# Two depthwise filters moved to 32x32 diagonal products on TensorE, in a layout of four bands of rows

## The chip, the cores and the metric

The kernel runs on one core of one Trainium2 chip. A core has TensorE (a matrix array that writes to PSUM), VectorE, ScalarE and GpSimd for elementwise work, and a sync queue that issues DMA transfers. In the profile they are PE (its weight loads PEld), DVE, ACT, POOL and SP. PSUM has eight banks of 512 f32 per partition. The metric is device time in microseconds (us), the median of several executions.

## The reference, cut to what matters

The input is 32 images of 56x56 pixels with 96 channels, f32. Four layers follow each other:

```python
# layer 0: mixture of 4 experts, weights mixed per image
h = relu(bn(x @ Wk + ...))             # 96 -> 384 channels
h = relu(bn(depthwise3x3(h) + ...))    # 384 channels
x = bn(h @ Wk2 + ...) + x              # 384 -> 96
# layer 1: depthwise 5x5 of 96 channels, added to its input
x = x + depthwise5x5(x, kernel)
# layer 2: relu, depthwise 3x3 of 96 channels, 96x96 product, batch norm
y = depthwise3x3(relu(x), dw_kernel) + dw_bias
x = bn(y @ pw_kernel + pw_bias)
# layer 3: shifted-window attention (7x7 windows, 3 heads of 32), then a
# perceptron 96 -> 384 -> 96 with gelu; layer norm before each, residual after
```

The change touches layers 1 and 2. A depthwise filter has no sum over channels: each channel is filtered by itself. On TensorE it can be written as one product per tap with a diagonal weight matrix, summed in PSUM.

## The kernel before

Each step of the outer loop works on three images at once; the generators hand over to each other at `yield`, in the proportion of their weights, and the scheduler places the instructions in that order of priority:

```python
for step in range(B + 2):
    # attention and perceptron of image step-2, weight 107
    # layers 1 and 2 of image step-1,           weight 44
    # layer 0 of image step,                    weight 42
    interleave(stages)
```

Layer 0 filters its 384 channels on VectorE, in six blocks (two halves of the rows, three groups of 128 channels):

```python
for t in range(9):                     # L320 on
    view = h1[:, dy : dy + HALF, dx : dx + W]
    if t == 0:
        nc.vector.tensor_scalar(acc, view, tap, None, ALU.mult)               # L324
    else:
        nc.vector.scalar_tensor_tensor(acc, view, tap, acc, ALU.mult, ALU.add)  # L326
nc.scalar.activation(h2[:, k], h2[:, k], AF.Relu, ...)                        # L329
```

After three blocks it makes the 384 -> 96 product (L344) and writes the image, with a border of zeros, to `x1`. Layers 1 and 2 of the image before it are then:

```python
def conv5(i):                          # 8 rows of layer 1
    pt = mm.tile([P, 512], F32, tag="mm", name="pt")
    o = pt[:C, : 8 * W].rearrange("c (r w) -> c r w", w=W)
    for t in range(25):
        dy, dx = divmod(t, 5)
        nc.tensor.matmul(o, diag5[:, t],                     # L368; diag5[:, t] is 96x96
                         x1[:, 8 * i + dy : 8 * i + dy + 8, dx : dx + W],
                         start=(t == 0), stop=(t == 24))
        if t % 5 == 4 and t < 24:
            yield
    nc.scalar.activation(x2[:, 1 + 8 * i : 9 + 8 * i, 1 : 1 + W], o, AF.Relu)   # L377

def filtered(i):                       # 7 rows of layer 2, on VectorE
    ...
    for t in range(9):
        if t == 0:
            nc.vector.tensor_scalar(acc, view, tap, None, ALU.mult)              # L390
        else:
            nc.vector.scalar_tensor_tensor(acc, view, tap, acc, ALU.mult, ALU.add)  # L392
    nc.gpsimd.tensor_copy(d[:, :, W:], d[:, :, :3])                              # L393
    nc.scalar.copy(dp, d[:, :, 3:].rearrange("c r (j w) -> c j r w", w=14))      # L395

def pointwise():                       # the 96x96 product and the bias
    ...                                # L402 on TensorE, L409 on VectorE
```

Attention works on eight groups of seven rows. For each group, `project` makes queries, keys and values (L478 to L490), `scores` takes three PSUM banks at once (L504), `probabilities` adds the mask on VectorE (L510), takes exponentials on ScalarE (L517) and divides on GpSimd (L521), `turned` transposes (L528), `weighted` multiplies with the values (L546), `attended` projects and adds (L554, L557). The perceptron follows (L570 to L585), and 17 output transfers a row group on the sync queue (L592 to L599). PSUM is shared out so:

```python
mm = ctx.enter_context(tc.tile_pool(name="mm", bufs=4, space=PSUM))    # all else
att = ctx.enter_context(tc.tile_pool(name="att", bufs=3, space=PSUM))  # scores, turned; and 1 "po"
```

Of the kernel before, what the change touches and what calls it, by code (L numbers as in the profile page):

```python
# [18 lines left out]
C = 96  # L19
# [7 lines left out]
NP = 4  # L27
NH = 3
# [30 lines left out]
def kernel(ctx: ExitStack, tc: tile.TileContext, a: dict, mask: bass.AP, out: bass.AP):  # L59
# [10 lines left out]
    att = ctx.enter_context(tc.tile_pool(name="att", bufs=3, space=PSUM))  # L70
# [4 lines left out]
    ones = const.tile([P, P], F32, name="ones")  # L75
# [83 lines left out]

    k5 = load([C, 25], a["L1_conv_kernel"].rearrange("c a b -> c (a b)"), "k5")  # L160
    nc.vector.tensor_scalar(k5[:, 12:13], k5[:, 12:13], 1.0, None, ALU.add)
    diag5 = const.tile([C, 25, C], F32, name="diag5")
    for t in range(25):
        nc.vector.tensor_scalar(diag5[:, t], ident[:C, :C], k5[:, t : t + 1], None, ALU.mult)
# [13 lines left out]
    nc.vector.tensor_scalar(dwb, ones[:C], col(U_DWB), None, ALU.mult)  # L178
# [22 lines left out]
    x2 = big.tile([C, H + 2, W + 2], F32, name="x2")  # L201
    nc.gpsimd.memset(x1, 0.0)
    nc.gpsimd.memset(x2, 0.0)


    consumed = [H]

    def stage_conditional(b):
# [5 lines left out]
        def load_rows(i):  # L214
            xin = work.tile([PK, NP, C], F32, tag="xin", name="xin", bufs=3)
            nc.sync.dma_start(
                out=xin,
                in_=x[b, 7 * i : 7 * i + 7].rearrange("r w c -> (r w) c").rearrange("(p j) c -> p j c", j=NP),
            )
            loaded.append(xin)  # L220
# [4 lines left out]
        for i in range(NROW):  # L225
            if i + 2 < NROW:
                load_rows(i + 2)
            xin = loaded[i]
            pt = mm.tile([P, 512], F32, tag="mm", name="pt")
            for j in range(NP):  # L230
                nc.tensor.transpose(pt[:C, j * PK : (j + 1) * PK], xin[:, j], ident[:PK, :PK])
            nc.scalar.activation(
                xT[:, i * RT : (i + 1) * RT].rearrange("c (p j) -> c j p", j=NP),
                pt[:C, :RT].rearrange("c (j p) -> c j p", j=NP),
                AF.Copy,
                accum_out=sums[:, i : i + 1],
            )
            yield
# [5 lines left out]
        nc.vector.tensor_scalar(pooled_w, ones[:C], pooled, 1.0 / (H * W), ALU.mult, ALU.mult)  # L244
# [69 lines left out]
        for at, (half, k) in enumerate(blocks):  # L314
# [22 lines left out]
            for n in range(4):  # L337
                r = half * HALF + 7 * n

                while consumed[0] < r + 7:  # L340
                    yield
# [19 lines left out]
    def stage_depthwise(b, res):  # L361

        def conv5(i):
            pt = mm.tile([P, 512], F32, tag="mm", name="pt")
            o = pt[:C, : 8 * W].rearrange("c (r w) -> c r w", w=W)
            for t in range(25):
                dy, dx = divmod(t, 5)
                nc.tensor.matmul(  # L368
                    o,
                    diag5[:, t],  # L370
                    x1[:, 8 * i + dy : 8 * i + dy + 8, dx : dx + W],
                    start=(t == 0),
                    stop=(t == 24),
                )
                if t % 5 == 4 and t < 24:
                    yield
            nc.scalar.activation(x2[:, 1 + 8 * i : 9 + 8 * i, 1 : 1 + W], o, AF.Relu)  # L377

        def filtered(i):
            d = work.tile([C, 7, W + 3], F32, tag="d", name="d")  # L380
            first = 7 * i + 3
            parts = ((0, first, 7),) if i < NROW - 1 else ((0, first, 4), (4, 0, 3))
            for to, r, n in parts:
                acc = d[:, to : to + n, :W]
                for t in range(9):
                    dy, dx = divmod(t, 3)
                    tap = col(U_DWK + t)
                    view = x2[:, r + dy : r + dy + n, dx : dx + W]
                    if t == 0:
                        nc.vector.tensor_scalar(acc, view, tap, None, ALU.mult)  # L390
                    else:
                        nc.vector.scalar_tensor_tensor(acc, view, tap, acc, ALU.mult, ALU.add)  # L392
            nc.gpsimd.tensor_copy(d[:, :, W:], d[:, :, :3])  # L393
            dp = work.tile([C, NP, 7, 14], F32, tag="dp", name="dp", bufs=1)
            nc.scalar.copy(dp, d[:, :, 3:].rearrange("c r (j w) -> c j r w", w=14))  # L395
            packed.append((i, dp))

        def pointwise():
            i, dp = packed.pop()
            pt = mm.tile([P, 512], F32, tag="mm", name="pt")  # L400
            for j in range(NP):
                nc.tensor.matmul(  # L402
                    pt[:PK, j * C : (j + 1) * C],
                    dp[:, j].rearrange("c r w -> c (r w)"),
                    pw,
                    start=True,
                    stop=True,
                )
            nc.vector.tensor_tensor(  # L409
                res[:, i],  # L410
                pt[:PK, : NP * C].rearrange("p (j c) -> p j c", c=C),
                bias2[:PK, None, :].to_broadcast([PK, NP, C]),
                ALU.add,
            )


        packed = []
        done = 0
        for i in range(7):
            for n, _ in enumerate(conv5(i)):  # L420
                yield
                if n == 1 and packed:
                    pointwise()

                    if 7 * done + 10 < 8 * i:
                        filtered(done)
                        done += 1
            consumed[0] = 8 * i + 6
            if packed:
                pointwise()  # L430
            if 7 * done + 10 < 8 * i + 8:
                filtered(done)
                done += 1
            yield
        consumed[0] = H
        while packed:
            for _ in range(4):
                yield
            pointwise()
            if done < NROW:  # L440
                filtered(done)
                done += 1
        assert done == NROW
# [25 lines left out]
    def stage_swin(b, res):  # L469
# [26 lines left out]
        def scores(i):  # L496

            qT, kT = rows_of[i][:2]
            pss = [att.tile([P, 512], F32, tag="att", name="ps") for _ in range(NH)]
# [7 lines left out]
        def probabilities(i, h):  # L507
            ps = scored[i][h]
            s = work.tile([PK, NP, PK], F32, tag="s", name="s", bufs=6)
# [14 lines left out]
        def turned(i, h):  # L524
            s = probs.pop((i, h))
            ps = att.tile([P, 512], F32, tag="att", name="ps")
# [9 lines left out]
        def weighted(i):  # L536

            v = rows_of[i][2]
            po = att.tile([P, 512], F32, tag="po", name="po", bufs=1)
# [105 lines left out]
    for step in range(B + 2):  # L645
# [3 lines left out]
        if 0 <= step - 1 < B:  # L649
            consumed[0] = 0  # L650
            residuals[step - 1] = two.tile([PK, NROW, NP, C], F32, tag="res", name="res")
            stages.append((stage_depthwise(step - 1, residuals[step - 1]), 44))
# [5 lines left out]
def build(nc, shapes, batch):  # L658

    a = {k: nc.dram_tensor(f"in_{k}", s, F32, kind="ExternalInput").ap() for k, s in shapes.items()}  # L660
    mask = nc.dram_tensor("in_mask", (2, PK, NP, PK), F32, kind="ExternalInput").ap()
    out = nc.dram_tensor("out", (batch, H, W, C), F32, kind="ExternalOutput").ap()
    with tile.TileContext(nc) as tc:
        kernel(tc, a, mask, out)
# [13 lines left out]
```

## Time and profile before

The time before is 9404.55 us (three runs, 9403.75 to 9406.23). The profiled execution spans 9402.1 us at a mean granted TensorE clock of 0.959.

| engine | busy us | share of the span | instructions |
|---|---|---|---|
| TensorE, products | 8762.3 | 93% | 47622 |
| TensorE, weight loads | 4987.7 | 53% | 47622 |
| VectorE | 7190.0 | 76% | 11221 |
| ScalarE | 4176.0 | 44% | 11520 |
| GpSimd | 3782.1 | 40% | 3406 |

Busy time is the time in which at least one instruction of the engine ran; loads overlap products. The chain of waits follows the program back from its last instruction, at each step to what released it, and says what share of the span each engine and line had on it. In a group line the figures after the bar are the busy time, the mean duration of one instruction in ns, and the idle time of the engine just before such instructions. One matrix product of f32 leaves two records of each kind. A steady step, from one image's first input transpose to the next one's, takes 287 us.

### The profile page before, as it was taken

Reading aid. Unit: us, or ns where it says so; the run is one execution under the profiler, and the core shown is the slowest. Engines: PE = TensorE matmul, PEld = TensorE weight load, DVE = VectorE, ACT = ScalarE, POOL = GpSimd, SP = SyncE. Lnnn points to the kernel's source line nnn. Section 1 sums busy time; section 2 is a strip of 40 time slices with the busy share of each in tenths; the row PEclk is TensorE's granted clock in tenths of the full one; section 3 lists DMA queues with packets and bytes.
Section 4 is the critical chain, followed back from the end, with each engine's and each line's share of the span. In section 5 each row is a group of like instructions: output and inputs, shape, how many; then the busy total and the mean of one; then the engine's idle time right before and its main releaser. Section 6 shows DMA issues by size and latency. Waiting matters only on the chain.

```text
span 9402.1 us, 132043 instructions
## 1 busy us (share of the span) xinstructions
PE 8762.3 (93%) x47622; PEld 4987.7 (53%) x47622; DVE 7190.0 (76%) x11221; ACT 4176.0 (44%) x11520; POOL 3782.1 (40%) x3406
## 2 busy tenths in 40 slices
PE   5899999999999999999999999999999999999998
PEld 2455555555555555555555555555555555555555
DVE  5778777788777787777887777877778877778754
ACT  2344444444444444444444444444444444444434
POOL 2244344444343443444443434434444434444333
PEclk8999999999999999999999999999999999999997
DMA  0000000000000000000000000000000000000000
GB/s 23 6 10 5 8 11 11 11 7 7 9 11 11 10 6 8 11 11 11 7 7 9 11 11 11 5 8 11 11 11 7 7 9 11 11 11 6 5 6 11
DMA packets 164927, 88.07 MB, mean 9 GB/s; under 512 B 138455, under 2 KB 164272, under 8 KB 164272
## 3 DMA queue, kind: packets, MB, share of 16 engines
q1 hardware_dynamic: 164272, 79.62, 3.3%
q8 instruction: 376, 6.16, 0.3%
q14 instruction: 279, 2.29, 0.1%
HBM read 40.95 MB, written 38.54 MB: 8 GB/s over the span
## 4 chain that ended last, share of the span: by engine, by line
PE 59%; DVE 26%; ACT 5%; POOL 4%; issue 3%; SPq 2%; DMA 0%; DVEq 0%; POOLq 0%; ACTq 0%
PE pt L368 30%; DVE h L326 18%; PE pt L344 5%; PE pt L577 4%; PE pt L570 4%; DVE d L392 2%; ACT s L517 2%; PE ps L504 2%; PE pt L402 2%; PE po L546 2%; PE pt L478 2%; PE pt L487 2%; PE pt L482 2%; PE pt L554 1%; PE ps L528 1%
## 5 line engine op out<-in xcount | busy, mean ns | idle before, releaser
L368 PE MATMUL pt<-x,diag 96*96 96x448 f32 x11200 | 4598.5, 552 | 44.6 <-ACT h L300 44.6
L326 DVE SCALAR_TENSOR_TENSOR h<-h,mix,h 128x1568 f32<-128x1568 f32 x1536 | 2840.7, 1860 | 4.3
L368 PEld LDWEIGHTS pt<-x,diag 96*96 96x96 f32 x11200 | 1742.6, 165 | 2000.9 <-issue 1898.8
L521 POOL TENSOR_TENSOR s<-s,den 98x392 f32<-98x392 f32 x768 | 996.1, 1299 | 1367.2 <-DVE den L520 1358.1
L392 DVE SCALAR_TENSOR_TENSOR d<-x,c,d 96x392 f32<-96x392 f32 (+2 forms) x2304 | 1446.6, 645 | 7.6 <-ACT x L377 1.3
L517 ACT ACTIVATE s<-s,top 98x98 f32<-98x98 f32 x3072 | 1118.1, 368 | 420.6 <-DVE top L514 420.0
L563 POOL TENSOR_TENSOR tb<-res,L_conv_b 98x384 f32<-98x384 f32 x256 | 655.7, 2561 | 1075.7 <-DVE res L557 678.4
L84 POOL TENSOR_TENSOR var<-var,mhalf 98x4 f32<-98x4 f32 x512 | 685.0, 1338 | 445.0 <-DVE var L83 427.7
L577 PEld LDWEIGHTS pt<-w,hid 128*98 128x98 f32 x6144 | 689.5, 189 | 207.9 <-ACT hid L571 117.2
L577 PE MATMUL pt<-w,hid 128*98 128x96 f32 x6144 | 710.7, 274 | 84.2 <-ACT hid L571 84.2
L492 POOL TENSOR_TENSOR xb<-res,L_conv_bo 98x384 f32<-98x384 f32 x256 | 386.7, 1511 | 833.7 <-DVE res L557 700.2
L570 PE MATMUL pt<-hT,w 96*128 96x392 f32 x1536 | 615.0, 540 | 106.4 <-ACT hT L466 106.4
L344 PE MATMUL pt<-h,wmix 128*96 128x392 f32 x1536 | 574.1, 504 | 60.6 <-ACT h L329 37.4
L293 PE MATMUL pt<-xT,wmix 96*128 96x392 f32 (+1 forms) x1536 | 591.2, 519 | 28.6 <-ACT h L300 24.4
L300 ACT ACTIVATE h<-pt,bias,s 128x392 f32<-128x392 f32 (+1 forms) x768 | 491.4, 686 | 272.3 <-PE pt L293 247.1
L466 ACT ACTIVATE hT<-pt,c 96x392 f32<-96x392 f32 x512 | 343.1, 670 | 593.2 <-PE pt L464 592.9
L517 ACT ACTIVATION_READ_ACCUMULATOR s<-s,top 98x1 f32 x3072 | 586.7, 191 | 0.0
L571 ACT ACTIVATE hid<-pt,c 128x392 f32<-128x392 f32 x768 | 444.3, 585 | 249.0 <-PE pt L570 215.9
L451 DVE TENSOR_TENSOR lnd<-res,mu 98x384 f32<-98x384 f32 x512 | 380.2, 743 | 218.4 <-PE pt L464 179.0
L457 POOL TENSOR_TENSOR lnd<-lnd,var 98x384 f32<-98x384 f32 x512 | 531.0, 1037 | 40.2
L510 DVE TENSOR_TENSOR s<-ps,masks 98x392 f32<-98x392 f32 x768 | 410.9, 553 | 177.2 <-PE ps L504 177.2
L329 ACT ACTIVATE h<-h,biasd,s 128x1568 f32<-128x1568 f32 x192 | 325.2, 1694 | 438.0 <-DVE h L326 438.0
(112 smaller groups left out, 10152.3 us busy)
## 6 DMA issues: line engine op xcount, KB each, us to landing
xin<-in_x SPq DMA_DIRECT2D x256, 147.0 KB
out<-o SPq DMA_DIRECT2D x1792, 4.1 KB
out<-o SPq DMA_DIRECT2D x1792, 1.1 KB
out<-o SPq DMA_DIRECT2D x672, 36.8 KB
out<-o SPq DMA_DIRECT2D x96, 21.0 KB
out<-o SPq DMA_DIRECT2D x96, 15.8 KB
wpw<-in_L_conv_Wpw SPq DMA_DIRECT2D x1, 576.0 KB
wpwl<-in_L_conv_Wpwl SPq DMA_DIRECT2D x4, 144.0 KB
```

The source lines that it names most:

```text
L84: nc.gpsimd.tensor_tensor(dst, dst, mhalf[:n, : dst.shape[1]], ALU.pow)
L293: nc.tensor.matmul(pt[:, : n * W], wmix[:, k * P : (k + 1) * P], xT[:, (first + r) * W : (first + r + n) * W], start=True, stop=True,)
L326: nc.vector.scalar_tensor_tensor(acc, view, tap, acc, ALU.mult, ALU.add)
L344: nc.tensor.matmul(pt[:C, :RT], wmix2[:, q * C : (q + 1) * C], h2[:, q, n * RT : (n + 1) * RT], start=(q == 0), stop=(q == NB - 1),)
L368: nc.tensor.matmul(o, diag5[:, t], x1[:, 8 * i + dy : 8 * i + dy + 8, dx : dx + W], start=(t == 0), stop=(t == 24),)
L392: nc.vector.scalar_tensor_tensor(acc, view, tap, acc, ALU.mult, ALU.add)
L457: nc.gpsimd.tensor_tensor(d, d, var[:, :, None].to_broadcast([PK, NP, C]), ALU.mult)
L517: nc.scalar.activation(s[:, j], s[:, j], AF.Exp, bias=top[:, j : j + 1], accum_out=den[:, j : j + 1])
L521: nc.gpsimd.tensor_tensor(s, s, den[:, :, None].to_broadcast([PK, NP, PK]), ALU.mult)
L563: nc.gpsimd.tensor_tensor(tb, res[:, i], b2[:PK, None, :].to_broadcast([PK, NP, C]), ALU.add)
L570: nc.tensor.matmul(pt[:, :RT], w1[:, k * P : (k + 1) * P], hT, start=True, stop=True)
L577: nc.tensor.matmul(pt[:PK, j * C : (j + 1) * C], hidden[k][:, j * PK : (j + 1) * PK], w2[:, k], start=(k == 0), stop=(k == NB - 1),)
```

## The change

It gives each 32x32 block of the matrix array its own small diagonal product, and lets the array hold twelve of them at a time. Layer 1 keeps its input `x1` with 96 channels on 96 partitions (three groups of 32). Its output goes to a new layout: the image is cut into four bands of 14 rows, and band b of each channel group goes to partitions 32b to 32b+31. So twelve products (three channel groups by four bands) use twelve blocks of the array. Layer 2 reads this layout, band by band, and brings the result back to 96 partitions, again with twelve blocks. Between the two, the rows at the band edges are copied to the neighbouring band by two DMA transfers. VectorE no longer takes part in the filter of layer 2. What it is for is to use the array's rows and columns, of which a 96x96 diagonal matrix uses only the diagonal, and to relieve VectorE.

The PSUM pools are cut anew: four banks for the filters, four for everything else, attention included. Layer 0 may write `x1` only when all of layer 1 is done, the weight of the middle stage falls from 44 to 26, and some buffers shrink (`xin` from 3 to 2, `s` from 6 to 5).

```diff
-    att = ctx.enter_context(tc.tile_pool(name="att", bufs=3, space=PSUM))
+    cv = ctx.enter_context(tc.tile_pool(name="cv", bufs=4, space=PSUM))
...
-    diag5 = const.tile([C, 25, C], F32, name="diag5")
+    diag5 = const.tile([C, 25, 32], F32, name="diag5")
...
-    x2 = big.tile([C, H + 2, W + 2], F32, name="x2")
+    x2 = big.tile([P, NG, BAND + 2, W + 2], F32, name="x2")
+    filtered = big.tile([C, NP, H + 3, 14], F32, name="filtered")
...
-                while consumed[0] < r + 7:
+                while not consumed[0]:
...
-        def conv5(i): ...
-        def filtered(i): ...
+        for u in range(2):
+            banks = [cv.tile([P, 512], F32, tag="cv", name="pc") for _ in range(NG)]
             for t in range(25):
                 dy, dx = divmod(t, 5)
+                for band in range(NBAND):
+                    r = BAND * band + 7 * u + dy
+                    for g in range(NG):
+                        gs = slice(32 * g, 32 * g + 32)
+                        nc.tensor.matmul(
+                            rows(banks[g], P)[32 * band : 32 * band + 32],
+                            diag5[gs, t],
+                            x1[gs, r : r + 7, dx : dx + W],
+                            start=(t == 0), stop=(t == 24),
+                        )
                 if t % 5 == 4 and t < 24:
                     yield
+            for g in range(NG):
+                nc.scalar.activation(x2[:, g, 1 + 7 * u : 8 + 7 * u, 1 : 1 + W], rows(banks[g], P), AF.Relu)
+            yield
+        consumed[0] = True
+        nc.sync.dma_start(out=x2[32:, :, 0], in_=x2[: P - 32, :, BAND])
+        nc.sync.dma_start(out=x2[: P - 32, :, BAND + 1], in_=x2[32:, :, 1])
+        for u in range(2):
+            banks = [cv.tile([P, 512], F32, tag="cv", name="pc") for _ in range(NBAND)]
+            for t in range(9):
+                ...
+                for g in range(NG):
+                    for band in range(NBAND):
+                        nc.tensor.matmul(
+                            rows(banks[band], P)[32 * g : 32 * g + 32],
+                            diag3[bs, g, t],
+                            x2[bs, g, r : r + 7, dx : dx + W],
+                            start=(t == 0), stop=(t == 8),
+                        )
+                if t % 3 == 2 and t < 8:
+                    yield
+            for band in range(NBAND):
+                ...                     # three nc.scalar.copy from banks[band] to filtered
+            yield
+        nc.gpsimd.tensor_copy(filtered[:, :, H:], filtered[:, :, :3])
+        yield
+        for i in range(NROW):           # the pointwise product, a yield after each
...
-            pss = [att.tile([P, 512], F32, tag="att", name="ps") for _ in range(NH)]
+            pss = [mm.tile([P, 512], F32, tag="mm", name="ps") for _ in range(NH)]
...
-            stages.append((stage_depthwise(step - 1, residuals[step - 1]), 44))
+            stages.append((stage_depthwise(step - 1, residuals[step - 1]), 26))
```

## The prediction

> **What bounds the kernel now.** I read the busy line first, then the chain of waits, then the costliest groups, then the time by stretches of one step. A step is one turn of the outer loop: attention and perceptron of image b-2, the two filters of image b-1, the first layer of image b.
>
> ```profile
> PE 8762.3 (93%) x47622; PEld 4987.7 (53%) x47622; DVE 7190.0 (76%) x11221; ACT 4176.0 (44%) x11520; POOL 3782.1 (40%) x3406
> ...
> PE 59%; DVE 26%; ACT 5%; POOL 4%; issue 3%; SPq 2%; DMA 0%; DVEq 0%; POOLq 0%; ACTq 0%
> PE pt L368 30%; DVE h L326 18%; PE pt L344 5%; PE pt L577 4%; PE pt L570 4%; DVE d L392 2%; ACT s L517 2%; PE ps L504 2%; PE pt L402 2%; PE po L546 2%; PE pt L478 2%; PE pt L487 2%; PE pt L482 2%; PE pt L554 1%; PE ps L528 1%
> ...
> L368 PE MATMUL pt<-x,diag 96*96 96x448 f32 x11200 | 4598.5, 552 | 44.6 <-ACT h L300 44.6
> L326 DVE SCALAR_TENSOR_TENSOR h<-h,mix,h 128x1568 f32<-128x1568 f32 x1536 | 2840.7, 1860 | 4.3
> ...
> L392 DVE SCALAR_TENSOR_TENSOR d<-x,c,d 96x392 f32<-96x392 f32 (+2 forms) x2304 | 1446.6, 645 | 7.6 <-ACT x L377 1.3
> ```
>
> TensorE is busy 93% and its layer-1 filter (L368) alone is 30% of the chain. But VectorE is second with 26%, nearly all of it the first layer's depthwise filter (L326), which the change leaves alone. The layer-2 filter that does leave VectorE (L392) is only 2% of the chain. So the bound changes hands within a step. The stretches show that (columns: stretch, length, then busy time and count of each engine, then granted TensorE clock, DMA share and GB/s):
>
> ```profile
> 28.00:167.00 139.00, 59.70 (x153) 30.22 (x152) 100.11 (x81) 37.05 (x55) 20.49 (x27) 0.74 0.03 9
> 167.00:380.00 213.00, 183.77 (x562) 85.61 (x561) 150.64 (x189) 48.41 (x76) 54.90 (x43) 0.91 0.02 6
> 4688.00:4736.00 48.00, 47.59 (x297) 26.50 (x296) 21.12 (x50) 29.29 (x109) 14.21 (x16) 1.00 0.09 26
> 4736.00:4901.00 165.00, 158.31 (x838) 83.78 (x837) 150.41 (x208) 72.84 (x205) 63.29 (x55) 0.98 0.00 1
> 4901.00:4975.00 74.00, 65.92 (x355) 44.73 (x355) 53.10 (x92) 28.24 (x49) 41.40 (x35) 0.92 0.07 17
> 8997.00:9224.00 227.00, 222.34 (x1336) 128.27 (x1336) 122.83 (x271) 92.89 (x303) 68.89 (x77) 0.99 0.02 5
> 9224.00:9402.00 178.00, 136.53 (x934) 101.65 (x932) 69.61 (x163) 84.72 (x285) 60.58 (x67) 0.65 0.04 9
> ```
>
> Rows 3 to 5 are one full step, 287 us: its start is TensorE alone, its middle has TensorE at 96% and VectorE at 91%, its end has neither full. Row 1 is the first layer alone (139 us, and VectorE-heavy), row 2 first layer and filters, row 6 filters and attention, row 7 attention and perceptron alone: 178 us although no engine is over 77%.
>
> **What the Trainium skill says.** Three places bear on it, and one warns. "TensorEngine Tiling (Array Packing)", Key Properties: different tiles load weights and multiply in parallel. "TensorE: Matmul & The Clock Gate", Measured speedup vs the span model: sixteen 32x32 tiles together ran 10.6 times as fast as one after another. The trace before agrees for three tiles, side by side in columns (L546) and in rows (L504):
>
> ```profile
> 5001.65 0.88 PE L546 MATMUL po<-pT,v 98*32 98x98 f32 x24
> 5002.45 4.03 PE L368 MATMUL pt<-x,diag 96*96 96x448 f32 x10
> ...
> 5007.44 0.94 PE L504 MATMUL ps<-kT,qT 32*98 32x98 f32 x24
> ```
>
> Each f32 product leaves two records. Ten L368 records run from 5002.45 to the next line's start at 5006.32, so one takes 387 ns, 0.864 ns a column. The 24 records of L546 are eight groups of three over 98 columns; the last lasts some 250 ns, so seven intervals fill 0.63 us: 90 ns, 0.92 ns a column for three tiles at once. Three tiles cost what one does. Twelve at once (rows times columns) no run here shows. Gotcha 1: PSUM Pressure, of the first page, says that row tiles must not write one PSUM bank together; the change gives each row group its own bank. The clock page's section What's actually happening warns that the clock halves when the array idles: row 7 shows 0.65, the full step 1.00 to 0.92.
>
> **The change part by part, per image.**
>
> 1. Layer-1 filter. Out: 4598.5/32 = 143.7 us of TensorE. In: 25 taps x 2 half-bands x 2 records = 100 waves of twelve tiles over 392 columns. At 0.864 x 392 = 339 ns a wave, 33.9 us.
> 2. Layer-2 filter. Out of VectorE: L392 1446.6 and its first tap L390 (165.8 in the groups by shape), together 1612/32 = 50.4 us. In on TensorE: 9 x 2 x 2 = 36 waves, 12.2 us. For filling and draining I add 0.25 us (one record's tail) for each of 16 bursts: 4 us.
> 3. ScalarE. Out: the relu L377 and the copy L395, (120.6+137.6)/32 = 8.1 us. In: six relus of 392 at about 0.6 (L300's 392 takes 0.69, L533's copy 0.48) and 24 copies, eight of 294 elements at 0.45 and sixteen of at most 77 at 0.33 (estimates from L533 and L517's 368 ns for 98): 12.5 us. Net +4.
> 4. Two halo transfers an image. The copies they need come after the last relu, and the program order has a projection, transposes and weighted sums on TensorE between the last layer-1 product and the first that waits for them. I count 0 to 3 us.
> 5. PSUM. Scores, transposes and weighted sums lose their four banks and share four with everything else; the filters take the other four.
>
> Sums of one step: TensorE 271.8-143.7+50 = 178 us, VectorE 224.6-50.4 = 174, ScalarE 130+4 = 135. If these overlapped perfectly the step would be near 180. They can't, because VectorE's L326 and L324, (2840.7+197.0)/32 = 95 us, stand in two clumps. So I dealt out the turns that the three generators take (107, 44, 42 before; 107, 26, 42 after), gave each turn the busy time of its rows, and cut the step by what the first layer does: A loading, B first three channel blocks, C outputs, D the other three blocks, E outputs and the rest. TensorE/VectorE in us, scaled by 0.90 and 0.93 so that the sums before are the measured busy times:
>
> - before: A 74/40, B 62/73, C 46/24, D 56/70, E 33/16. The larger ones add up to 296; measured 287, so the rule reads 3% high.
> - after: A 51/35, B 42/61, C 23/12 (ScalarE 26 is the largest), D 34/61, E 34/11. The larger ones: 51+61+26+61+34 = 233, less 3% = 226.
>
> To that I add 5 us, my choice, for shared PSUM and for waits that layer-1 products used to cover: **231 us a step**. The whole: 167 to the end of the first image's first layer (start 28 + row 1, unchanged); the next step 150 (row 1 plus a little, its 213 was TensorE); 30 full steps x 231 = 6930; filters with attention 180 (row 7's length, as TensorE's 222 falls by 94); row 7 unchanged 178. Sum 7605, rounded to **7600 us**.
>
> **Rivals.**
>
> - *VectorE becomes the bound and hides most of the gain.* This is part of my sum: B and D stay at 61 each. If all slack of TensorE were gained and VectorE never waited, a step would be 190 and the whole about 6400. Against that speaks row 7: attention alone is held by its own chain of waits.
> - *Twelve tiles don't run together.* If only six did, the filters would take 46 us more on TensorE; that falls on A and C, 25 to 35 us a step, whole about 8500. If only three did, the filters would cost about as much as before, and only VectorE's 50 us would be won: 9000 or a little over. For it: nothing here shows more than three. Against it: rows and columns each show no loss at three, and the skill's sixteen.
> - *PSUM becomes the wait.* One step takes about 185 tiles from those four banks (96 in attention, 40 in the perceptron, 41 in the first layer, 8 in the pointwise product). In 231 us that is 5.0 us a tile; a tile needs about 0.7 of writing and 0.6 of reading, plus its wait behind VectorE's operations of 1.86 us. Three banks at once for scores make it tight. A further 20 us a step would give 8200.
> - *The clock halves.* TensorE will be full about 77% of a step. In B and D a halved clock would be hidden behind VectorE, in A and E not: up to 15 us a step.
> - *Output issues on the sync queue.* A row group's 17 output transfers hold that queue 7.8 us, so 62 us an image; the perceptron's stretch is 74 us. It can shrink little, and my E and D together (95 us) leave room.
>
> **Range and chances.** A step of 213 (little loss to PSUM, some smoothing across the parts) gives about 7050; one of 252 (PSUM and clock both bite, or tiles overlap in part) about 8250. Faster by over 2% would fail only if tiles ran three or four at a time: 0.04 slower, 0.03 the same, 0.93 faster.
>
> **What would show each step right or wrong.** The new filter lines on TensorE should be busy about 1100 and 390 us, together under 1700; over 2500 would mean that tiles queue. VectorE should be busy near 5580. In a full step VectorE should be near 100% in two stretches of some 60 us, and on the chain L326's successor should lead, with over 25%. If waits of TensorE for VectorE's mask addition or copies lead the waits, PSUM is the rival that won; if the clock in full steps is under 0.85, the clock is. The prediction is wrong altogether if a wave of twelve takes far more than 339 ns.

## The result and the profile after

The changed kernel takes **9085.8 us** (9082.6 to 9091.9, four runs) against 9404.3 (9403.8 to 9406.2, four runs): 0.966 of the time before, interval 0.9645 to 0.9678. The gain is 319 us. Predicted was 7600, with 8250 as the upper end of the range, so more than four fifths of the expected gain are missing.

The page of the changed kernel has these lines in the places of those shown of before: busy time, chain by engine, chain by line, and three of the costliest groups. In the new file L347 is layer 0's taps (before L326), L396 the layer-1 products (before L368), and L423 the layer-2 products, which take the place of VectorE's L392.

```profile
PE 7756.6 (85%) x88646; PEld 4572.9 (50%) x88646; DVE 5804.0 (64%) x8611; ACT 4125.0 (45%) x12000; POOL 3442.0 (38%) x3182
...
PE 48%; DVE 31%; ACT 11%; POOL 4%; issue 4%; SPq 1%; DMA 0%; ACTq 0%; DVEq 0%; POOLq 0%
DVE h L347 21%; PE pc L396 11%; PE pt L588 7%; ACT s L535 6%; PE pt L365 5%; PE pt L595 5%; PE pc L423 3%; PE pt L314 3%; DVE s L528 2%; POOL var L87 2%; PE pt L572 2%; PE pt L505 2%; PE pt L496 2%; DVE h L345 2%; PE pt L448 2%
...
L347 DVE SCALAR_TENSOR_TENSOR h<-h,mix,h 128x1568 f32<-128x1568 f32 x1536 | 2889.5, 1903 | 5.2 <-DVE den L538 0.5
L396 PE MATMUL pc<-x,diag 32*32 32x392 f32 x38400 | 2109.7, 572 | 11.7 <-ACT x L406 6.6
...
L423 PE MATMUL pc<-x,diag 32*32 32x392 f32 x13824 | 711.8, 573 | 6.0 <-ACT filtered L440 3.8
```

VectorE fell by 1386 us, as it should (5804; predicted 5580). TensorE fell by only 1006, although the filters were to save some 3000. Two readings follow from these lines. First, the filters are busy 2109.7 + 711.8 = 2822 us, 88 us an image and not 50. Second, take the filters off the engine's sum: (7756.6 - 2821.5)/32 = **154 us** an image of other products, where before it was (8762.3 - 4598.5)/32 = **130 us**. The change doesn't touch those products, and they cost 24 us more.

Where in the run the prediction missed is in the stretches (stretch, length, busy time and count of each engine, granted clock, DMA share, GB/s). The rows are the first image's layer 0, the second step, 30 full steps, and the end:

```profile
28.00:161.50 133.50, 54.17 (x152) 26.69 (x150) 100.20 (x81) 37.37 (x55) 16.64 (x26) 0.73 0.03 9
161.50:332.00 170.50, 120.78 (x1949) 69.45 (x1947) 110.86 (x108) 46.08 (x91) 44.47 (x38) 0.82 0.03 9
332.00:8694.00 8362.00, 7249.00 (x82946) 4248.51 (x82945) 5431.06 (x8028) 3856.96 (x11241) 3232.75 (x2957) 0.85 0.04 11
8694.00:9090.00 396.00, 330.63 (x3602) 226.63 (x3600) 156.39 (x365) 183.32 (x614) 129.97 (x143) 0.77 0.04 9
```

The steps hold nearly the whole miss: 8362 where 30 x 231 = 6930 was predicted. The start is 332 for 317 and the end 396 for 358. So the question is one step: 279 us for 231.

One full step of before, then one of after, each cut as in the prediction into A to E (loading, three blocks of taps, layer 0's outputs, three blocks, the rest). The second and fourth number of a row's busy times are weight loads and ScalarE, the fifth GpSimd:

```profile
4687.70:4749.30 61.60, 61.13 (x374) 33.67 (x373) 34.42 (x87) 33.26 (x116) 15.84 (x18) 1.00 0.07 21
4749.30:4822.40 73.10, 69.29 (x369) 36.98 (x368) 70.28 (x80) 35.72 (x109) 31.60 (x24) 0.95 0.00 1
4822.40:4859.50 37.10, 37.02 (x207) 19.55 (x206) 27.43 (x60) 17.50 (x65) 16.97 (x20) 1.00 0.00 0
4859.50:4926.60 67.10, 61.25 (x313) 35.67 (x310) 63.99 (x60) 25.56 (x39) 29.13 (x20) 0.97 0.02 5
4926.60:4976.30 49.70, 44.73 (x233) 29.87 (x234) 28.52 (x66) 18.33 (x34) 25.35 (x26) 0.90 0.08 19
```

```profile
4796.10:4856.90 60.80, 59.24 (x995) 35.84 (x994) 28.63 (x77) 33.48 (x119) 16.40 (x19) 0.92 0.09 24
4856.90:4919.10 62.20, 52.52 (x610) 25.72 (x609) 58.15 (x57) 26.39 (x75) 26.49 (x21) 0.73 0.01 2
4919.10:4967.30 48.20, 43.86 (x565) 24.01 (x566) 18.21 (x43) 26.12 (x106) 16.03 (x19) 0.89 0.01 2
4967.30:5036.90 69.60, 48.76 (x307) 32.63 (x306) 61.55 (x57) 27.45 (x53) 30.57 (x23) 0.81 0.04 9
5036.90:5076.00 39.10, 38.94 (x302) 24.08 (x301) 14.67 (x38) 15.43 (x27) 18.49 (x19) 0.94 0.07 16
```

Of the parts, only B is as predicted (62 for 61). A is 10 us too long, C 22, D 9 and E 5. In A, C and E TensorE is busy 91 to 100% of the time, so there the miss is TensorE's. In B and D VectorE is busy 93 and 88%, and it is there that the granted clock drops most: 0.73 and 0.81, where before it was 0.95 and 0.97.

### The profile page after: what moved, and what is told of

Read it like the earlier page. It is cut to its first block, busy times and chain, and to the rows that moved or that the text cites. A ratio compares the mean times of both kernels' runs of the same rounds, so it can differ in the third digit from the quotient of the medians.

```text
span 9090.1 us, 213022 instructions
## 1 busy us (share of the span) xinstructions
PE 7756.6 (85%) x88646; PEld 4572.9 (50%) x88646; DVE 5804.0 (64%) x8611; ACT 4125.0 (45%) x12000; POOL 3442.0 (38%) x3182
## 4 chain that ended last, share of the span: by engine, by line
PE 48%; DVE 31%; ACT 11%; POOL 4%; issue 4%; SPq 1%; DMA 0%; ACTq 0%; DVEq 0%; POOLq 0%
DVE h L347 21%; PE pc L396 11%; PE pt L588 7%; ACT s L535 6%; PE pt L365 5%; PE pt L595 5%; PE pc L423 3%; PE pt L314 3%; DVE s L528 2%; POOL var L87 2%; PE pt L572 2%; PE pt L505 2%; PE pt L496 2%; DVE h L345 2%; PE pt L448 2%
## 5 line engine op out<-in xcount | busy, mean ns | idle before, releaser
L347 DVE SCALAR_TENSOR_TENSOR h<-h,mix,h 128x1568 f32<-128x1568 f32 x1536 | 2889.5, 1903 | 5.2 <-DVE den L538 0.5
L396 PE MATMUL pc<-x,diag 32*32 32x392 f32 x38400 | 2109.7, 572 | 11.7 <-ACT x L406 6.6
L396 PEld LDWEIGHTS pc<-x,diag 32*32 32x32 f32 x38400 | 875.4, 113 | 689.2 <-issue 449.0
L87 POOL TENSOR_TENSOR var<-var,mhalf 98x4 f32<-98x4 f32 x512 | 747.0, 1459 | 937.0 <-DVE var L86 878.9
L588 PE MATMUL pt<-hT,w 96*128 96x392 f32 x1536 | 758.9, 643 | 121.8 <-ACT hT L484 121.7
L314 PE MATMUL pt<-xT,wmix 96*128 96x392 f32 (+1 forms) x1536 | 708.4, 590 | 130.3 <-DVE res L575 56.0
L365 PE MATMUL pt<-h,wmix 128*96 128x392 f32 x1536 | 628.2, 546 | 122.6 <-ACT pT L551 67.0
L423 PE MATMUL pc<-x,diag 32*32 32x392 f32 x13824 | 711.8, 573 | 6.0 <-ACT filtered L440 3.8
L581 POOL TENSOR_TENSOR tb<-res,L_conv_b 98x384 f32<-98x384 f32 x256 | 510.3, 1993 | 483.1 <-DVE res L575 381.4
L321 ACT ACTIVATE h<-pt,bias,s 128x392 f32<-128x392 f32 (+1 forms) x768 | 481.9, 691 | 393.7 <-PE pt L314 388.5
L575 DVE TENSOR_TENSOR res<-pt,xb 98x384 f32<-98x384 f32 x256 | 141.3, 552 | 801.0 <-PE pt L572 801.0
L510 POOL TENSOR_TENSOR xb<-res,L_conv_bo 98x384 f32<-98x384 f32 x256 | 332.2, 1298 | 844.2 <-DVE res L575 649.9
L350 ACT ACTIVATE h<-h,biasd,s 128x1568 f32<-128x1568 f32 x192 | 324.4, 1690 | 646.3 <-DVE h L347 646.3
L588 PEld LDWEIGHTS pt<-hT,w 96*128 96x128 f32 x1536 | 345.2, 239 | 421.1 <-ACT hT L484 183.4
```

The costliest lines, as they stand in the source:

```text
L87: nc.gpsimd.tensor_tensor(dst, dst, mhalf[:n, : dst.shape[1]], ALU.pow)
L314: nc.tensor.matmul(pt[:, : n * W], wmix[:, k * P : (k + 1) * P], xT[:, (first + r) * W : (first + r + n) * W], start=True, stop=True,)
L365: nc.tensor.matmul(pt[:C, :RT], wmix2[:, q * C : (q + 1) * C], h2[:, q, n * RT : (n + 1) * RT], start=(q == 0), stop=(q == NB - 1),)
L396: nc.tensor.matmul(rows(banks[g], P)[32 * band : 32 * band + 32], diag5[gs, t], x1[gs, r : r + 7, dx : dx + W], start=(t == 0), stop=(t == ...
L423: nc.tensor.matmul(rows(banks[band], P)[32 * g : 32 * g + 32], diag3[bs, g, t], x2[bs, g, r : r + 7, dx : dx + W], start=(t == 0), stop=(t ...
L581: nc.gpsimd.tensor_tensor(tb, res[:, i], b2[:PK, None, :].to_broadcast([PK, NP, C]), ALU.add)
```

## The experiments

Three explanations of the missing gain were on the table: PSUM's shared banks, the twelve tiles and the order of the products, and TensorE's clock together with VectorE's clump of taps. All times but those of the two kernels and of the last version are one execution each; executions of one kernel agree within 0.3% here, so differences under 30 us are not read.

### PSUM: the bank layout without the new filters

The kernel before, with attention's banks merged into the shared pool and the layer-1 filter given four banks of its own, as the change divides them:

```diff
-    att = ctx.enter_context(tc.tile_pool(name="att", bufs=3, space=PSUM))
+    cv = ctx.enter_context(tc.tile_pool(name="cv", bufs=4, space=PSUM))
-            pss = [att.tile([P, 512], F32, tag="att", name="ps") for _ in range(NH)]
+            pss = [mm.tile([P, 512], F32, tag="mm", name="ps") for _ in range(NH)]
...                        # ps and po in the same way; the layer-1 filter's pt from cv
```

> The kernel before, with only the PSUM split of the change: scores, transposes and weighted sums share the four banks of everything else, the 96x96 filter of layer 1 has four banks of its own. Nothing is left out. If the shared banks are what ate the gain (theory PSUM), some 20 to 40 us a step are lost here too: 10000 to 10600 us. If the gain was lost to lone products and the order on TensorE (theory order), or to the clock, this stays within 2% of before: 9300 to 9600 us.

Measured 9225.9 us: 178 us *faster* than before, outside both expected ranges. In the kernel before, the new division costs nothing on balance. Of the 319 us that the whole change wins, the re-division of banks would have won 178; the step went from 287 to about 283 us and the second step from 213 to 170. If the two parts simply add, the new filters themselves won some 140.

It does not follow that shared banks cost nothing in the changed kernel. TensorE's longest wait there, and the next, are:

```profile
PE pt L572 <- ACT h L321: 261.2, 30, 8.7
PE po L564 <- DVE pT L549: 221.4, 60, 6.6
```

The first comes once a step and is a wait for a shared bank, as part D of the step above shows on TensorE and ScalarE:

```profile
4979.35 1.68 PE L314 MATMUL pt<-xT,wmix 96*128 96x448 f32 x4
...
4982.66 1.63 PE L314 MATMUL pt<-xT,wmix 96*128 96x392 f32 x4
4993.01 1.64 PE L572 MATMUL pt<-wo,oT 96*98 96x96 f32 x8 [8.72 <-ACT h L321]
...
4982.84 0.48 ACT L569 COPY oT<-po 96x392 f32<-96x392 f32 x1 [4.11 <-PE po L564]
4990.65 1.69 ACT L350 ACTIVATE h<-h,biasd,s 128x1568 f32<-128x1568 f32 x1 [7.33 <-DVE h L347]
4992.25 2.41 ACT L321 ACTIVATE h<-pt,bias,s 128x448 f32<-128x448 f32 x4
```

Layer 0's four products (L314, two records each) fill all four banks. ScalarE reads them (L321) only after its instruction in front of that (L350) has waited 7.33 us for VectorE's taps. Attention's output product (L572) has had its operand since 4983.3 and waits 8.72 us for a bank. In the run of this experiment, with the 96x96 filter, the two longest such waits add up to 55 and 36 us. So the rival of PSUM is refuted as a cost of the bank division by itself, not as a wait in the changed kernel; what one bank more would win there no run shows.

### The filters: what is left when they are nearly gone

One tap of each filter (leaves out 24 of 25 and 8 of 9), in the scheduler's order; the stage still hands over as often as before:

```diff
-            for t in range(25):
+            for t in (12,):
...
-            for t in range(9):
+            for t in (4,):
```

> The changed kernel with one tap of 25 in layer 1 and one of 9 in layer 2; the other 24 and 8 are left out, everything else stays, so 88 us a step of TensorE's filter work fall to some 4 to 6. Theory order (the filter products, in pieces, are still on the path): at least 30 us a step less, under 8200 us. Theory PSUM or a VectorE and attention chain that holds the step: the filters are off the path already, and it stays over 8700 us.

Measured 8375.5 us, between the two expectations, clock 0.703:

```profile
PE 6442.9 (77%) x39494; PEld 4129.3 (49%) x39494; DVE 5755.2 (69%) x8611; ACT 4124.6 (49%) x12000; POOL 3676.8 (44%) x3182
```

The filters' busy time fell from 88 to 19 us an image, 69 less; a steady step fell from 279 to 257, 22 less. The other products grew in the same run: (6442.9 - 618.0)/32 = 182 us, after 154. This is the run that pointed to the clock.

### The order of the products

In the scheduler's order the bursts of the filters don't stay whole. The timeline of the changed kernel on TensorE shows what that costs (start, length, line, count of records; each product leaves two):

```profile
4797.69 3.80 PE L396 MATMUL pc<-x,diag 32*32 32x392 f32 x116
4801.42 0.54 PE L482 MATMUL pt<-ident,lnd 98*96 98x98 f32 x4
4801.79 0.50 PE L250 MATMUL pt<-ident,xin 98*96 98x98 f32 x4
4802.22 0.84 PE L396 MATMUL pc<-x,diag 32*32 32x392 f32 x2
...
4875.07 1.51 PE L396 MATMUL pc<-x,diag 32*32 32x392 f32 x2
...
4877.95 6.79 PE L396 MATMUL pc<-x,diag 32*32 32x392 f32 x118
```

A piece of 116 records takes 3.73 us up to the next line's start, 32 ns a record. One product (two records) that the scheduler dealt out alone takes 0.84 us, as much as 26 records in a burst. The last two rows are the same two things at half clock: 1.51 and 6.79. Counted from the starts of all records, an image has 25 such small pieces (102 records of 1632), and they take 25 us of TensorE, idle time left out.

To keep the bursts whole, TensorE's instructions were held to the order in which the program emits them:

```diff
-        interleave(stages)
+        with tc.manual_schedule(engines={mybir.EngineType.PE}):
+            interleave(stages)
```

> The changed kernel with TensorE's instructions held to the order in which the program emits them, so that bursts of 60 and 36 products stay whole and no product of a filter stands alone; all other engines are ordered by the scheduler. Theory order: the filters fall from 88 us a step to 50 to 60, lone products vanish, 15 to 30 us a step are won: 8150 to 8600 us. Theory PSUM or clock: within 2% of 9086, or slower, since a fixed order can make TensorE wait.

> Control: the kernel before with TensorE held to the emitted order in the same way. If a fixed order is good in itself, this wins as much as the changed kernel does with it. Theory order says that only packed products suffer from being pulled apart (a lone one takes as long as twelve), so this stays within 2% of 9404: 9250 to 9600 us.

Measured 8893.0 us for the changed kernel, 193 less, and 9916.2 for the kernel before, 512 more. Both missed their ranges: the first won 7 us a step where order alone was to win 15 to 30, the second lost over 5% where it was to stay within 2. So it isn't that this order is good in itself: it is worse for the kernel before, and better for the one whose packed bursts the scheduler splits.

```profile
L396 PE MATMUL pc<-x,diag 32*32 32x392 f32 x38400 | 1644.8, 568 | 48.2 <-POOL x L374 48.2
...
L423 PE MATMUL pc<-x,diag 32*32 32x392 f32 x13824 | 634.8, 625 | 24.4 <-DMA x<-x 19.9
```

The filters fell from 88 to (1644.8 + 634.8)/32 = 71 us an image, the others stayed (157). TensorE has 14 us less to do, and a steady step is only 7 shorter (279 to 272).

Larger and smaller pieces, both with TensorE in emitted order: all 25 taps in one burst of 300 products (layer 2's nine in one of 108), or one tap (12 products) at a time with the stage's weight raised to match.

```diff
-                if t % 5 == 4 and t < 24:
-                    yield
+                if t == 24:            # the large pieces; the small ones: if t < 24: yield
+                    for _ in range(4):
+                        yield
```

> As a_pe, with the filters in bursts as long as they can be: all 25 taps of a half band (300 products, some 17 us at 28 ns a record) and all 9 taps of layer 2 (108, 6 us) without a break; the number of turns is the same. The other end from a_fine_pe (12 products; 9762 us, clock 0.741). The filters' own time falls from 73 us a step to 50 to 55. Theory burst length: fewer starts, and the array is warm within a burst: 8400 to 8850 us. Theory clock: between the bursts there is nothing left to hold the clock, it falls below 0.80, and what the bursts win the rest loses: 8850 to 9300 us.

> As a_pe, and the filters give way after every tap (12 products, 24 records, some 0.7 us) instead of after 5 or 3 taps; the weight of that stage becomes 100 for its 77 turns, so that it still ends in time. The same products in smaller pieces, closer together. Theory clock (the granted clock falls whenever no dense products come for a few us): the clock of 0.852 moves clearly, and the time with it, up to 0.92 and 8500 us or, if pieces of 0.7 us are too thin to count, down below 0.8 and over 9000 us. Theory clumps, or the filters' own length: clock about as before, time within 1.5% of 8893, a little more for 52 more starts of 0.2 us each (10 us a step, up to 9200).

Measured 9342.0 and 9762.3 us. The large bursts have the cheapest filters of all, 58 us an image, and yet lose 449 us to pieces of 60, as the clock falls to 0.780, the other products grow to 176 us and TensorE idles 8 us an image longer. The small pieces lose on both: filters 89, others 173, clock 0.741. Of the three sizes the middle one is best, and what puts it ahead of the large is not the filters' own cost.

### VectorE's clump

Layer 0 with three of its nine taps (leaves out six), still three hand-overs a block, TensorE in emitted order:

```diff
-            for t in range(9):
+            for t in (0, 5, 8):
                 dy, dx = divmod(t, 3)
                 tap = mix[:, k, t : t + 1]
```

> As a_pe, with three of the nine taps of layer 0 on VectorE; six are left out in each of six blocks, 6 x 6 x 1.9 = 67 us of VectorE work a step. If VectorE's taps hold parts B and D (62 and 65 us in a_pe), a step falls by 35 to 60 us: 7000 to 7800 us. If TensorE, slowed by its clock, or attention's own chain is the bound close behind, only 10 to 30 us a step: 7900 to 8600 us.

Measured 7905.4 us. A steady step takes 243 us for 272, 29 less for 64 us of VectorE work less (busy 5812 to 3756.5 us an execution). VectorE does hold the step, but with less than half of what the taps weigh: this is the second expectation, in which another bound stands close behind. How VectorE holds TensorE is visible in the changed kernel's timeline at 5146 us. Four taps run in a row, 8.21 us, and a copy of transposed probabilities comes after them; TensorE's weighted sum waits for that copy (in brackets: idle time before, and its releaser):

```profile
5146.02 8.21 DVE L347 SCALAR_TENSOR_TENSOR h<-h,mix,h 128x1568 f32<-128x1568 f32 x4
5154.15 0.55 DVE L549 COPY pT<-ps 98x392 f32<-98x392 f32 x1
...
5154.76 0.54 PE L564 MATMUL po<-pT,v 98*32 98x98 f32 x4 [6.54 <-DVE pT L549]
```

Spreading the taps (a hand-over after every one, weight 42 to 78), the same with the small pieces, and VectorE, or all four engines, held to emitted order too:

> As a_pe (8893 us, TensorE in the emitted order), and layer 0 gives way after each of its nine VectorE taps instead of every third (its weight 42 becomes 78), so that its 95 us of VectorE work stand in about 70% of a step instead of 43%. Theory clumps (in the parts where the taps stand VectorE holds everything, 62 and 65 us, and the other parts are TensorE's): the parts level out, a step falls by 15 to 40 us, to 7700 to 8450 us. Theory clock (TensorE at half clock is the bound anyway): within 2% of 8893.

> Both edits together. If clumps of VectorE work and the clock each cost by themselves, the two gains add: below the better of the two single runs by at least 100 us. If levelling VectorE already keeps TensorE fed (and so its clock up), the second edit adds nothing: within 1% of the better one.

> As a_pe (8893 us), and VectorE too is held to the emitted order: never more than three taps of layer 0 in a row (six at two places a step), attention's operations between them, where the scheduler's order has runs of eight and taps ahead of attention. Theory VectorE order (attention falls behind in part B, 62 us, and is made up in part C, 49 us against my 26): 10 to 30 us a step less, 8000 to 8600 us. Theory clock and burst length: VectorE's order is of no account, within 2% of 8893.

> The changed kernel with TensorE, VectorE, ScalarE and GpSimd all in the emitted order. If the scheduler's estimate of packed products (each taken as if it ran alone) is what places everything wrongly, this is as good as a_pedve or better, under 8600 us. If the scheduler's order on ScalarE and GpSimd hides waits, this is slower than a_pe: 8900 to 9500 us.

Measured 9282.8, 9893.2, 11011.5 and 11437.4 us. None helps, and no expected gain came. A fixed order makes VectorE wait 1590 us for ScalarE's exponentials in the third of these. No order that was tried dissolves the clump at a profit.

### Useless products to hold the clock

24 products that are written to spare banks and never read, before each of the eight pointwise products (TensorE in emitted order):

> As a_pe, with work added that is of no use: before each of the eight pointwise products of an image 24 more filter products (48 records, 1.3 us) are made into filter banks that nobody reads. It is 11 us a step of added TensorE work, in the part after the filters, where the clock is 0.84 and TensorE has 15 us of slack. Theory clock: the clock there rises above 0.9 and the time does not rise, or falls, to 8600 to 8900 us. If the clock doesn't matter: 0 to 11 us a step more, 8900 to 9220 us.

Measured 9442.3 us, above both ranges, clock 0.865. The padding is busy 570 us, 18 an image, and a steady step grew by the same 18 us (272 to 290). Filters fell to 64 us, the other products stayed at 157. What was added is paid in full.

### The square: filters and taps, each present or not

Still open was whether the other products grow through the clock itself or only because TensorE waits for VectorE. The run with one tap of each filter was repeated in emitted order, and once more with three taps in layer 0; with two earlier runs that makes a square.

> The changed kernel with one tap of each filter (leaves out 24 of 25 and 8 of 9) and TensorE in emitted order. Against the changed kernel in that order (8893, filters 70 us a step, other products 158 at clock 0.85) about 56 us a step of filter work go. Theory, the clock: the other products grow to about 180 us a step and the clock falls to about 0.70, so the step shortens by some 25 us only and the time is near 8200 (8000 to 8450). Rival, TensorE is a plain sum: the whole 56 us come off, near 7150. Rival, VectorE alone sets the step: little comes off, near 8700.

> The same with three of nine layer-0 taps as well (leaves out 6), which takes about 68 us a step from VectorE. It makes a square of four kernels with the two that leave out one of the two and the one that leaves out neither (8893, 7905). Theory, the clock and VectorE's clump are two separate losses: each takes its own stretches, so the time is near the sum of both savings, 7200 (7000 to 7450), with the clock near 0.72 and the other products still 175 us a step or more. Rival, the clock falls only because TensorE waits for VectorE: with the clump gone the clock comes back over 0.85, the other products fall to about 145 and the time goes under 6700. Rival, the other products are slow only through their own order: 0.70 and 180 whether VectorE is free or not, and the time over 7500.

| TensorE in emitted order | us | filters, us an image | other products | clock |
|---|---|---|---|---|
| all taps | 8893 | 71 | 157 | 0.852 |
| one tap of each filter | 7962 | 8 | 177 | 0.749 |
| three of nine layer-0 taps | 7905 | 66 | 149 | 0.907 |
| both | 7079 | 9 | 180 | 0.752 |

One tap of each filter came out just under the range of its theory (8000), both edits within theirs. The savings nearly add: 931 and 988 each alone, 1814 together. So they are in the main two separate losses; not wholly, as the clock rises from 0.852 to 0.907 when taps alone go. It is 0.75 without the filters whether VectorE is busy or not, and the other products grow by 20 us with the full taps and by 31 with three. With VectorE out of the way TensorE is even fuller, and still slow.

Whether the growth is the clock can be counted: in the traces every moment is granted 1.00 or 0.50, and busy time at 0.50 can be taken at half. Then the other products weigh 134 to 135 us an image in the first three rows of the table and 132 in the last, and 132 in the changed kernel as the scheduler orders it. So the spread from 149 to 180 is the clock's. Against the kernel before it is only part: there they weigh 123, with 14 us busy at half clock where the changed kernel has 44. Of the 24 us of growth, 15 are the clock and 9 are not. Counted from the start of one record to that of the next, the 9 are 5, so part of them is only how overlapping records are counted; what makes the rest stays open.

In the run with both edits, the busy line, one group and three stretches read:

```profile
PE 6036.3 (85%) x39494; PEld 4042.4 (57%) x39494; DVE 3695.3 (52%) x7459; ACT 4139.7 (58%) x12000; POOL 2839.8 (40%) x3182
...
L314 PE MATMUL pt<-xT,wmix 96*128 96x392 f32 (+1 forms) x1536 | 925.9, 767 | 42.9 <-ACT hT L483 22.2
...
5000.00:5010.00 10.00, 9.26 (x64) 6.94 (x66) 2.65 (x6) 4.11 (x13) 3.10 (x4) 0.50 0.08 25
5010.00:5020.00 10.00, 9.45 (x74) 6.05 (x71) 5.47 (x15) 7.67 (x33) 2.41 (x3) 0.50 0.17 48
5020.00:5030.00 10.00, 9.43 (x73) 7.18 (x71) 7.88 (x28) 3.82 (x9) 1.84 (x2) 0.50 0.04 7
```

The granted clock is 0.50 for 30 us in which TensorE is busy 93 to 95%. L314's record takes 767 ns here; in the changed kernel in emitted order it takes 636, with three layer-0 taps 584. What one product pays when the clock halves is in the chain of waits of the changed kernel, where the same six records of L588 come twice, first at a granted clock of 0.50, then at 1.00:

```profile
5311.62 4.29 PE pt L588 x6
...
5333.69 2.17 PE pt L588 x6
```

### The place in the step, and the best version

Weight of the stage of layers 1 and 2 raised from 26 to 32 (bursts earlier) or lowered to 21 (later), TensorE in emitted order:

> The changed kernel with TensorE in emitted order and the weight of the stage of layers 1 and 2 raised from 26 to 32: all filter bursts are whole as at weight 26, but end earlier in the step, and layer 0's outputs wait less for them. Theory, the placing of the bursts matters through the clock: earlier bursts leave the late part of the step at half clock, 9000 to 9300. Rival, layer 0's outputs wait for the filters in the third part of the step: under 8800.

> The changed kernel with TensorE in emitted order and the weight of the stage of layers 1 and 2 lowered from 26 to 21, so that its whole bursts lie later in the step; the opposite of weight 32, which took 9136 against 8893 at weight 26. Theory, the loss at weight 32 is one of placement alone and weight 26 is already near the best place: 8950 to 9250, with the clock still near 0.85. Rival, later bursts are better still, as dense work then covers the end of the step: under 8850.

Measured 9136.2 us at 32 and 9020.0 at 21, against 8893 at 26. The clock hardly moves (0.845 and 0.839 for 0.852), so here it is not the clock, and that 9136 lies in the range of the clock theory is luck. At 32 the fixed order puts TensorE behind layer norms that GpSimd hasn't finished:

```profile
PE pt L482 <- POOL lnd L475: 340.0, 61, 8.2
```

At weight 26 that wait was 45.3 us in all. At 21 it is layer 0's first products (L314) that wait, 279 us for L321 and 239 for L575. So the weight seems to matter through what stands next to what, and 26 is the best of the three.

The version with whole bursts beats both kernels and was timed in rounds:

> The changed kernel with TensorE in emitted order again, timed in rounds, as the version that beats both: 8893 in one look, so 0.945 to 0.947 of the kernel before.

Measured **8900.1 us** (8899.1 to 8905.0, four runs), 0.946 of the kernel before, interval 0.9449 to 0.9480.

## Why the prediction was wrong, point by point

- **Part 1 and 2, the wave: right.** In the 300-product bursts successive dozens of records follow each other after 334 ns at full clock (median of some 1300, most within 328 to 338) and 653 at half, counted from the starts of the records; 339 was predicted. Twelve tiles run together, and that rival is refuted. Its sign did come up, filters busy 2822 us where over 2500 "would mean that tiles queue"; the next two points say why. It was also priced wrongly: three tiles at a time would make 136 x 4 x 339 ns = 184 us an image, not "about as much" as the 144 of before.
- **The 50 us that the filters were to cost: wrong, it is 88.** The term took all 136 waves in unbroken bursts at full clock, plus 4 us. By the starts of the records, in the changed kernel: records in large pieces at full clock take 33.5 ns, so 1632 would take 54.7 us. The small pieces add 22 us, large pieces at half clock 9 (86 together by this count, 88 on the page). Holding the order takes 17 of the 22 away (88 to 71 us on the page).
- **The 128 us left of TensorE (271.8 - 143.7): wrong, it is 154.** That subtraction assumed that the same instructions would cost the same. Before, the filter was 30% of the chain, and the clock was 0.96 with it. With it shortened the clock fell to 0.85 and the rest took longer; the square shows the same step further on (0.75, 177 to 180 us). By the count above the clock makes 15 of the 24 us between 130 and 154. Both corrections together bring TensorE's 178 us a step to 242, 64 more, where the step is 48 longer than predicted.
- **The rival "the clock halves": right in kind, wrong in size and place.** Its sign, a clock under 0.85 in full steps, was at its mark with 0.85. It was given up to 15 us a step, in A and E, and "hidden behind VectorE" in B and D. The other products' growth through it alone is 15 us, and the filters lose more; the clock is lowest in B and D, and it isn't hidden there: attention falls behind while TensorE is slow, and its products come in C, D and E, where TensorE is then the bound. That the work is carried over in this way is only read from C, 48 us for 26, of which 17.6 are layer-2 filters; no run isolates it.
- **The rule of the larger sum per part: failed at C and D.** It had read 3% high before, and it let each part hold the work that the turns deal it. With VectorE full in B and TensorE waiting (3.46 us busy in 10, at 5146 to 5156), the parts aren't independent. VectorE's own sum was good: 181 us in the step shown, for 174. On the chain its taps lead with 21%, where over 25 were expected; the reading that they were "nearly all" of VectorE's 26% before was too high, they were 18.
- **PSUM: not settled.** I added a part of 5 us a step for it, and named a further 20 as a rival. By themselves, in the kernel before, the re-divided banks were worth -178 us of the whole; why the layer-1 filter's own banks help was not tested. In the changed kernel one wait for a bank is 261 us, 8.7 a step, and how much of it lengthens the step no run shows.
- **Output issues: as said.** The sync queue has 1% of the chain. The end is 396 us for 358, at a clock of 0.77.

Two places of the Trainium skill are to be read again with these numbers. "TensorE: Matmul & The Clock Gate", What's actually happening, says that the clock follows how busy the array has been of late. The runs agree that it moves between full and half, but the profile's busy time is no measure of that: it shows 93 to 95% at 0.50. In those 30 us TensorE works on attention, transposes and layer 0's first products. In that run attention's scores start at half clock in 73% of their records and its output product in 75%, but the perceptron's second product only in 7% and layer 0's output product in 5%. So without the filters it is attention's part of the step that loses the clock, not every other product. Within the filters' long pieces it comes back: in the changed kernel 148 of them begin at half clock, and all but one end at full. By which rule the hardware counts, no run here shows. "TensorEngine Tiling (Array Packing)", Key Properties, has tiles load and multiply in parallel, and the 334 ns agree; but that holds only while the tiles stand next to each other in the queue, and a tile alone costs 0.84 us.

## What to carry to other kernels

Before shortening TensorE's largest dense group, ask what it does for the clock: take the granted clock of a stretch of the same kernel without it (here 0.65 at the end of the run before), and price all other products there. When packing small tiles, look after scheduling whether the tiles still stand together, and compare the price of a piece of two records with that of a whole burst. And test each side effect of a change alone: here the re-division of PSUM, made in the kernel before, won more than half of what the whole change won.

## What of the hardware was not expected

- A lone 32x32 product over 392 columns takes 0.84 us at full clock and 1.51 at half, as much as thirteen products (26 records) of a burst at the same clock.
- The clock stays at 0.50 for tens of us with TensorE 93 to 95% busy.
- With the bursts whole, one of 120 records at full clock takes 3.89 us up to the next line's start, and 10 waves at 334 ns would be 3.34: starting and ending a burst costs about 0.5 us, not the 0.25 that was estimated.
